# Parting the mixture's weights beside later attention heads, in a fixed place of each

## The chip, the cores and the metric

The kernel runs on one core of a Trainium2 chip. The metric is the device time of one execution in microseconds. Beside it stand profiles: one execution recorded by the hardware profiler, with the start and end of every instruction of each engine. PE is the matrix engine (PEld its weight loads), DVE the vector engine, ACT the scalar engine, POOL GpSimd, and SP the sync engine, which here only issues DMA transfers. Each engine takes its instructions from a queue of its own, in the order that the program gives it.

## The reference

The function is one transformer block with adaptive layer norm. `x` has 4 sequences of 512 tokens with 256 features.

```python
mod = (_silu(L0_c) @ L0_wmod).reshape(L0_c.shape[0], 6, 1, -1)
sa, ca, ga, sb, cb, gb = ...           # shifts, scales and gates of the two halves
h = _layernorm(x) * (1 + ca) + sa
x = x + ga * attention(h)              # 16 causal heads of 128, softmax in float32
h = _layernorm(x) * (1 + cb) + sb
x = x + gb * ffn(h)                    # 8 experts, top 2 by a router, and a shared one
```

The attention has 64 (sequence, head) pairs. The mixture of experts (`ffn`) takes `h` down to 128 features, sends every token through two of eight two-layer experts with hidden sizes of 128 to 512, adds a shared expert and a dense core, and goes back up to 256. All is float32.

## The kernel before, in words

**Float32 products in three passes.** A float32 operand is parted into a high part that the fast matmul format (`float32r`) holds and the rest: `hi = copy(a)`, `lo = a - hi`. A product is then three matmuls into one PSUM bank (`mm3`, lines 138 to 142: weights' rest, moving operand's rest, both high parts). Everything that meets a matmul this way is parted first: ACT copies, DVE or POOL subtracts (`rest`, line 148, so all subtractions carry that line and are told apart by their tiles).

**The attention loop** (lines 1028 to 1093) runs over the 64 pairs; index `n` is called a head here. Groups of four heads of one sequence follow each other: heads 0 to 3 are sequence 0, 4 to 7 sequence 1, and so on; heads 16 to 31 are the second group of weights. In head `n` the loop writes down

- the scores of the four token tiles (`weights`, lines 471 to 504). For each tile PE writes `ps` (lines 482 and 140 to 142), DVE masks it and finds the row's extreme (L488, which frees the PSUM bank; there are two of them), ACT takes the exponential (L498), DVE the reciprocal of the sum (L502), POOL multiplies by it (L503). The function hands out the instructions of each tile: `exp` is the exponential, `by_sum` the multiplication. Those of the fourth tile are the head's last.
- between the tiles, the projections `pq` and `pk` of the next head (`project`), then the values `pv` (`values`);
- the attention weights of this head transposed by DVE (L512, L518), four DMAs to DRAM (`moved`, L524) and one back (`aT`, L528);
- those of head `n - 2` parted (`parted`: ACT copies `aTh`, L535; POOL subtracts), those of head `n - 3` multiplied with the values (`pz`, then `zh` and `zl`), and those of head `n - 4` projected out (`po`).

**Weights of the attention** are loaded as they are needed (`load_unit`, lines 185 to 196): a DMA (L188) into a staging buffer, POOL copies (L194) and subtracts. The heads of sequence 3 load the query, key and value weights of the next group (heads 12 to 15, 28 to 31, 44 to 47); heads 16, 18, 32, 34, 48 and 50 load output weights.

**Weights of the mixture** are parted ahead, during the attention. There are 11 units of up to 128 x 512 (`TO_PART`: five "first", three "second", shared, core, down). `stage_wf` (lines 221 to 224) loads a unit by one to three DMAs (L182). `part_wf` (lines 226 to 237) parts it: an ACT copy into a second buffer (L234), a POOL subtraction in place (L148), and a DMA of each result to DRAM (L235, L237); a "second" unit is first also stored whole (L232), since the subtraction overwrites it. The parts are loaded back near the end of the attention. `PART_AT` says in which head a unit is parted; it is staged one head earlier.

**Buffers.** The staging tag "stage" has two buffers of 128 x 512 floats. `load_unit`'s block, a unit's block, and the unit's high part take them in turn, in the order in which the program writes them down. One comes free when its last reader is done: for a parted unit, when the DMA of the part has landed.

**What sets the order.** PE's queue follows the program's text. For the other engines a planner sorts the instructions at build time, by a simulated timeline: an instruction is put into its engine's queue where the simulation has the engine free and the operands ready, earlier text first. It can so stand well ahead of its place in the text. Two things hold it: data and buffers, and `tc.issue_after(i)`, under which every instruction written in the block is queued behind `i`, if it runs on `i`'s engine. Instructions of other engines in the block, DMAs of SP among them, are not held. At run time each queue is worked off in its order: an instruction that waits holds back what is queued behind it.

In the traced program L234 is the ACT copy of a unit; the first three run at 40 to 60 us, during heads 2 to 4, though the text has them at heads 7, 9 and 11.

Of the kernel before, what the change touches and what calls it, by code (L numbers as in the profile page):

```python
# [98 lines left out]


TO_PART = tuple(u for u, (_, in_parts) in UNITS.items() if in_parts)
PART_AT = (7, 9, 11, 20, 22, 24, 26, 36, 38, 40, 42)

LATE_UNITS = (
    ("first3", "wu", 0),
# [8 lines left out]
def adaln_attention_moe_kernel(  # L114
# [29 lines left out]
    def f32(a: bass.AP) -> bass.AP:  # L144
        return a.bitcast(F32)

    def rest(eng, lo, full, hi):
        return eng.tensor_tensor(lo, full, f32(hi), ALU.subtract)  # L148
# [30 lines left out]
    def load_runs(to: bass.AP, src: list):  # L179
        at = 0  # L180
        for a in src:
            nc.sync.dma_start(to[:, at : at + a.shape[-1]], a)  # L182
            at += a.shape[-1]

    def load_unit(src, nm: str, early: bool = False):

        st = work.tile([P, 512], F32, tag="stage", name=f"st_{nm}")
        nc.sync.dma_start(st, src)  # L188
        u = const.tile([P, 2, 512], F32R, tag="wu", name=nm, bufs=10)
        hi, lo = u[:, 0], u[:, 1]  # L190
        if early:
            nc.scalar.copy(hi, st)
        else:
            nc.gpsimd.tensor_scalar(hi, st, 1.0, 1.0, ALU.mult, ALU.mult)  # L194
        rest(nc.gpsimd, lo, st, hi)
        return hi, lo
# [19 lines left out]
    def wf_runs(u: str):  # L216
        return [wf[:, at * P : (at + n) * P] for at, n in runs(UNITS[u][0])]
# [3 lines left out]
    def stage_wf(u: str):  # L221
        n = len(UNITS[u][0]) * P
        staged[u] = work.tile([P, 512], F32, tag="stage", name=f"st_wf_{u}")[:, :n]
        load_runs(staged[u], wf_runs(u))

    def part_wf(u: str):

        n = len(UNITS[u][0]) * P
        st = staged[u]
        d = parts_d[u] = dram.tile([P, 3, n], F32, tag=f"wfp_{u}", name=f"wfp_{u}")  # L230
        if u.startswith("second"):
            nc.sync.dma_start(d[:, 2, :], st)  # L232
        hi = work.tile([P, 512], F32R, tag="stage", name=f"hi_wf_{u}")[:, :n]
        nc.scalar.copy(hi, st)  # L234
        nc.sync.dma_start(d[:, 0, :], f32(hi))  # L235
        rest(nc.gpsimd, st.bitcast(F32R), st, hi)
        nc.sync.dma_start(d[:, 1, :], st)  # L237
# [171 lines left out]
    def norm_batch(b: int, which: int):  # L409
        if which and b > 1:  # L410
            with tc.issue_after(recent["hidden"]):
                xns[b, which] = normed(b, which)
            return
        xns[b, which] = normed(b, which)
# [56 lines left out]
    def weights(b: int, h: int, q, k):  # L471


        e = work.tile([P, E_END], F32, tag="e", name=f"e_{b}_{h}")
        nm = small.tile([P, NT], F32, tag="nmax", name=f"nmax_{b}_{h}", bufs=4)
        tot = small.tile([P, NT], F32, tag="tot", name=f"tot_{b}_{h}", bufs=4)
        inv = small.tile([P, NT], F32, tag="inv", name=f"inv_{b}_{h}", bufs=4)
        for t in range(NT):
            n = (t + 1) * P
            ps = psum.tile([P, S], F32, tag="sc", name=f"ps_{b}_{h}_{t}")  # L480
            if t == 0:
                nc.tensor.matmul(ps[:, :n], lhsT=q[0], rhs=k[0], start=True, stop=True)  # L482
            else:
                at = ts(t - 1, P)
                mm3(ps[:, :n], (q[1][:, at], q[2][:, at]), (k[1][:, :n], k[2][:, :n]), True, True)
            et = e[:, E_AT[t] : E_AT[t] + n]

            least = nc.vector.tensor_tensor_reduce(  # L488
                out=et,
                in0=ps[:, :n],  # L490
                in1=maskf[:, S - n :],
                scale=-SCALE,
                scalar=BIG,
                op0=ALU.add,
                op1=ALU.min,
                accum_out=nm[:, t : t + 1],
            )
            exp = nc.scalar.activation(  # L498
                et, et, AF.Exp, bias=nm[:, t : t + 1], scale=-1.0, accum_out=tot[:, t : t + 1]
            )  # L500
            one = slice(t, t + 1)
            nc.vector.reciprocal(inv[:, one], tot[:, one])  # L502
            by_sum = nc.gpsimd.tensor_scalar(et, et, inv[:, one], 1.0, ALU.mult, ALU.mult)  # L503
            yield e, least.ins, exp.ins, by_sum.ins

    def turned(b: int, h: int, e):


        tb = work.tile([P, NB, X], F32, tag="T", name=f"T_{b}_{h}")
        blocks = e.rearrange("p (n i s) -> p n i s", i=NB, s=R)  # L510
        to = tb.rearrange("p i (n r) -> p n i r", r=R)
        nc.vector.transpose(to[:, 0], blocks[:, E_AT[0] // P])  # L512
        for c in range(NT):
            t = max(c, 1)
            n = NT - t
            first = PAIR_AT[c] + t - c
            at, step = E_AT[t] // P + c, E_STEP // P
            nc.vector.transpose(  # L518
                to[:, first : first + n], blocks[:, at : at + (n - 1) * step + 1 : step]
            )  # L520

        moved = dram.tile([NB, R, NB, X], F32, tag="moved", name=f"moved_{b}_{h}")
        for a in range(NB):
            nc.sync.dma_start(  # L524
                moved[:, :, a, :].rearrange("i s x -> s i x"), tb[a * R : (a + 1) * R]
            )
        aT = work.tile([P, NB, X], F32, tag="aT", name=f"aT_{b}_{h}", bufs=3)
        nc.sync.dma_start(aT, moved.rearrange("i s a x -> (i s) a x"))  # L528
        return aT
# [460 lines left out]
    def modulate(b: int, which: int):  # L990

        m = modulated(b, which)
        next(m)
        begun_norms.append(m)
# [33 lines left out]
    for n, (b, h) in enumerate(order):  # L1028
        scores = weights(b, h, q, k)
        nb, nh = order[n + 1] if n + 1 < N else (None, None)  # L1030
        next(scores)
        _, least, *_ = next(scores)

        if n < HG * (B - 1):
            if h == 0:
                with tc.issue_after(least):
                    norm_batch(b + 1, 0)
            if h == 2:
                modulate(b + 1, 0)
        if b == 0 and h < HG:  # L1040
            if h + 2 < HG:
                wqk_u[h + 2] = load_unit(wqk[h + 2], f"wqk{h + 2}")
            if h == 0:
                wv_u[1] = load_unit(wv[1], "wv1")
            if h in (1, 2):
                wo_u[h - 1] = load_unit(wo[h - 1], f"wo{h - 1}")
        for f, *args in later.pop(n, ()):
            f(*args)
        if n + 1 in PART_AT:
            stage_wf(TO_PART[PART_AT.index(n + 1)])  # L1050
        if n in PART_AT:
            part_wf(TO_PART[PART_AT.index(n)])
        if nb is not None:
            q = project(nb, nh, 0)
        next(scores)
        if nb is not None:
            k = project(nb, nh, 1)
        end_norm()
        e, _, exp, by_sum = next(scores)
        if len(waiting) > 1:  # L1060
            part_one(-2)
        if h % 2 == 0:
            values(b, h // 2, 1)
        elif nb is not None:
            values(nb, nh // 2, 0)
        else:
            last_exps["head"] = exp
            prepared[0] = before_chunks(0)
        if done:
            finish(n, *done.pop())  # L1070
        if len(waiting) == LAG:
            db, dh, aT = waiting.pop(0)
            done.append((db, dh, mixed(db, dh, aT)))
        with ExitStack() as after:
            if nb is None:
                after.enter_context(tc.issue_after(begun[0]))
            waiting.append((b, h, turned(b, h, e)))

        with tc.issue_after(by_sum):
            if b == B - 1 and h + HG < H:  # L1080
                wqk_u[h + HG] = load_unit(wqk[h + HG], f"wqk{h + HG}")
                if h % 2 == 0:
                    wv_u[(h + HG) // 2] = load_unit(wv[(h + HG) // 2], f"wv{(h + HG) // 2}")
            if b == 0 and h >= HG and h % 2 == 0:
                wo_u[h // 2] = load_unit(wo[h // 2], f"wo{h // 2}")
            if b == B - 1 and h + HG >= H:
                for u in (
                    ("down", "first0"),
                    ("whole", "second0"),
                    ("first1",),  # L1090
                    ("first2", "second1"),
                )[h + HG - H]:
                    load_wf(u)
# [6 lines left out]
    n = N  # L1100
# [97 lines left out]
```

## Time and profile before

| | |
|---|---|
| median of 3 runs | 817.98 us (817.22 to 819.26) |
| profiled execution | 815.89 us |
| its span, from the first to the last instruction | 814.1 us |
| mean granted clock of TensorE | 0.989 |
| busy: PE, DVE, ACT, POOL | 776.6, 596.6, 490.1, 520.6 us |
| a head with PE busy throughout (heads 24 to 34) | 9.19 us |
| DMA, hardware queue: share of the 16 engines' time, bytes moved | 52.4%, 123.21 MB |
| `moved` to landing, `aT` to landing (medians) | 2.8 and 4.0 us |

A profile's page gives the busy time of each engine, the waits between engines, and the chain of work that ended last. A table by stretches gives the same busy times for a part of the span, and a timeline the single instructions. In a line of waits, "A <- B: 8.8, 2, 4.5" says that A waited for B for 8.8 us in all, twice, 4.5 us at most. In a line of the timeline the first number is the start in us from the beginning of the span, the second the duration, and in brackets stands the engine's idle time before it and what ended it. Idle time of an engine that is not the bound costs nothing by itself.

The attention fills the first 628 us or so, the mixture of experts the rest.

### The profile page before, as it was taken

The numbers are of one execution on the slowest core, as the hardware profiler recorded it, in microseconds if no ns is written. First come the engines' busy times: TensorE is split into PE (matmuls) and PEld (weight loads), VectorE is DVE, ScalarE is ACT, GpSimd is POOL, SyncE is SP. The second block draws the span as 40 slices with busy tenths as digits, with TensorE's granted clock in tenths as the row PEclk, the third lists the DMA queues.
The fourth block names the chain that finished last, engine by engine and source line by source line (L and its number), as shares of the span: only waits on it lengthen the run. The fifth ranks groups of instructions, "written<-read, shape, count | busy, mean of one in ns | idle before, by whom it ended". The sixth has DMA issues, their size and how long they took to land.

```text
span 814.1 us, 14111 instructions
## 1 busy us (share of the span) xinstructions
PE 776.6 (95%) x4487; PEld 671.2 (82%) x4487; DVE 596.6 (73%) x1734; ACT 490.1 (60%) x1184; POOL 520.6 (64%) x523
## 2 busy tenths in 40 slices
PE   6898999999999999999999999999998998989997
PEld 5677898999978999998899999999887766767775
DVE  5976888777657777766777677778898587795555
ACT  3575667666656765665666666666656334656663
POOL 4665566896756688675656886656556245565675
PEclk9999999999999999999999999999999899999999
DMA  7376454665775456657555675644576333322221
GB/s 234 102 254 190 130 156 132 183 184 155 219 229 158 135 171 186 179 159 209 160 145 159 174 194 146 186 132 140 153 195 206 105 123 85 101 57 74 57 82 61
DMA packets 73218, 124.12 MB, mean 152 GB/s; under 512 B 8996, under 2 KB 51252, under 8 KB 73144
## 3 DMA queue, kind: packets, MB, share of 16 engines
q1 hardware_dynamic: 73112, 123.21, 52.4%
q8 instruction: 36, 0.59, 0.3%
q14 instruction: 38, 0.31, 0.1%
q0 software_dynamic: 32, 0.02, 0.0%
HBM read 73.05 MB, written 50.14 MB: 151 GB/s over the span
## 4 chain that ended last, share of the span: by engine, by line
PE 72%; DVE 10%; DMA 7%; POOL 4%; ACT 2%; issue 2%; SPq 2%; DVEq 0%; ACTq 0%; POOLq 0%
PE acc L835 4%; PE ps L140 3%; PE pz L140 3%; PE pz L141 3%; PE pz L142 3%; PE ps L141 3%; PE ps L142 3%; PE po L140 3%; PE po L141 3%; PE po L142 3%; PE pk L141 3%; PE pk L140 3%; PE pk L142 3%; PE pv L140 3%; PE pv L142 3%; PE pv L141 3%
## 5 line engine op out<-in xcount | busy, mean ns | idle before, releaser
L148 POOL TENSOR_TENSOR aT<-aT,aTh 128x1152 fp32r<-128x1152 f32 x64 | 172.0, 2687 | 109.0 <-ACT aTh L535 105.9
L503 POOL TENSOR_SCALAR e<-e,inv 128x128 f32<-128x128 f32 (+3 forms) x256 | 135.1, 542 | 68.7 <-DVE inv L502 66.2
L498 ACT ACTIVATE e<-e,nmax 128x128 f32<-128x128 f32 (+3 forms) x256 | 143.3, 561 | 49.7 <-DVE nmax L488 48.9
L535 ACT CAST aTh<-aT 128x1152 fp32r<-128x1152 f32 x64 | 74.0, 1157 | 122.8 <-DMA aT<-moved 61.9
L488 DVE CUSTOM_DVE_ANT_0 e<-ps,mask 128x128 f32<-128x128 f32 (+3 forms) x256 | 120.3, 478 | 28.6 <-PE ps L482 17.8
L518 DVE STREAM_TRANSPOSE T<-e 128x384 f32<-128x384 f32 (+2 forms) x256 | 100.5, 445 | 10.2 <-POOL e L503 10.1
L140 PE MATMUL ps<-kh,ql 128*128 128x256 f32 (+2 forms) x192 | 71.6, 373 | 12.4 <-DVE nmax L488 12.4
L148 DVE TENSOR_TENSOR zl<-pz,zh 128x512 fp32r<-128x512 f32 x64 | 43.9, 687 | 48.9 <-ACT zh L553 48.2
L140 PE MATMUL po<-wo,zl 128*128 128x256 f32 x256 | 73.1, 286 | 1.0 <-DVE zl L148 1.0
L140 PE MATMUL pv<-wv,hTl 128*128 128x256 f32 x256 | 72.0, 281 | 0.5 <-DVE hTl L148 0.5
L141 PE MATMUL po<-wo,zh 128*128 128x256 f32 x256 | 72.1, 282 | 0.0
L142 PE MATMUL po<-wo,zh 128*128 128x256 f32 x256 | 72.0, 281 | 0.0
L141 PE MATMUL pv<-wv,hTh 128*128 128x256 f32 x256 | 71.5, 279 | 0.0
L142 PE MATMUL pv<-wv,hTh 128*128 128x256 f32 x256 | 71.5, 279 | 0.0
L502 DVE RECIPROCAL inv<-tot 128x1 f32<-128x1 f32 x256 | 40.2, 158 | 40.8 <-ACT e L498 33.6
L863 POOL TENSOR_TENSOR oacc<-oacc,part 128x512 f32<-128x512 f32 x28 | 40.9, 1461 | 43.4 <-DVE part L859 36.5
L141 PE MATMUL ps<-kl,qh 128*128 128x256 f32 (+2 forms) x192 | 65.4, 340 | 0.3 <-DVE kl L148 0.3
L140 PE MATMUL pz<-aTh,vl 128*128 128x512 f32 (+2 forms) x192 | 65.0, 339 | 0.0
L141 PE MATMUL pz<-aT,vh 128*128 128x512 f32 (+2 forms) x192 | 64.9, 338 | 0.0
L142 PE MATMUL ps<-kh,qh 128*128 128x256 f32 (+2 forms) x192 | 64.9, 338 | 0.0
L142 PE MATMUL pz<-aTh,vh 128*128 128x512 f32 (+2 forms) x192 | 64.9, 338 | 0.0
L140 PEld LDWEIGHTS ps<-kh,ql 128*128 128x128 f32 x192 | 36.5, 190 | 22.3 <-DVE nmax L488 15.3
(216 smaller groups left out, 2332.1 us busy)
## 6 DMA issues: line engine op xcount, KB each, us to landing
moved<-T SPq DMA_DIRECT2D x256, 160.0 KB, 2.8
aT<-moved SPq DMA_DIRECT2D x64, 640.0 KB, 4.0
spread<-gates_e SPq DMA_DIRECT2D x32, 256.0 KB, 3.3
st_wqk<-in_wqk SPq DMA_DIRECT2D x16, 256.0 KB, 3.7
wf_first<-wfp_first SPq DMA_DIRECT2D x5, 512.0 KB, 4.7
st_wv<-in_wv SPq DMA_DIRECT2D x8, 256.0 KB, 3.3
st_wo<-in_wo SPq DMA_DIRECT2D x8, 256.0 KB, 3.4
wmod<-in_wmod SPq DMA_DIRECT2D x6, 256.0 KB, 5.6
```

What stands on the lines that cost most here:

```text
L140: nc.tensor.matmul(o, lhsT=wl, rhs=mh, start=start, stop=False)
L141: nc.tensor.matmul(o, lhsT=wh, rhs=ml, start=False, stop=False)
L142: nc.tensor.matmul(o, lhsT=wh, rhs=mh, start=False, stop=stop)
L148: return eng.tensor_tensor(lo, full, f32(hi), ALU.subtract)
L488: least = nc.vector.tensor_tensor_reduce(out=et, in0=ps[:, :n], in1=maskf[:, S - n :], scale=-SCALE, scalar=BIG, op0=ALU.add, op1=ALU.min, ...
L498: exp = nc.scalar.activation(et, et, AF.Exp, bias=nm[:, t : t + 1], scale=-1.0, accum_out=tot[:, t : t + 1])
L502: nc.vector.reciprocal(inv[:, one], tot[:, one])
L503: by_sum = nc.gpsimd.tensor_scalar(et, et, inv[:, one], 1.0, ALU.mult, ALU.mult)
L518: nc.vector.transpose(to[:, first : first + n], blocks[:, at : at + (n - 1) * step + 1 : step])
L535: nc.scalar.copy(hi, full)
L835: nc.tensor.matmul(acc, lhsT=w2(k, b), rhs=act[:, s], start=c == 0, stop=c == n - 1)
L863: recent["added"] = nc.gpsimd.tensor_tensor(oacc, oacc, to, ALU.add).ins
```

## The change

The list of heads in which units are parted changes from 7, 9, 11, 20, 22, 24, 26, 36, 38, 40, 42 to 18, 20, 22, 24, 26, 28, 34, 36, 38, 40, 42. The first three partings leave the first twelve heads; two come to heads 18 and 28 and one to head 34, and the units move along in their order.

The two calls move within the head's text, from ahead of the next head's query projection to behind the DVE transposes of the head's own weights. They stand under two `issue_after`: the ACT copy is queued behind the head's last exponential, the POOL subtraction behind the head's last normalisation. The DMAs of staging and storing are held by neither, since they run on SP.

```diff
-PART_AT = (7, 9, 11, 20, 22, 24, 26, 36, 38, 40, 42)
+PART_AT = (18, 20, 22, 24, 26, 28, 34, 36, 38, 40, 42)
...
         for f, *args in later.pop(n, ()):
             f(*args)
-        if n + 1 in PART_AT:
-            stage_wf(TO_PART[PART_AT.index(n + 1)])
-        if n in PART_AT:
-            part_wf(TO_PART[PART_AT.index(n)])
         if nb is not None:
             q = project(nb, nh, 0)
...
             waiting.append((b, h, turned(b, h, e)))
+
+        with tc.issue_after(by_sum), tc.issue_after(exp):
+            if n + 1 in PART_AT:
+                stage_wf(TO_PART[PART_AT.index(n + 1)])
+            if n in PART_AT:
+                part_wf(TO_PART[PART_AT.index(n)])
 
         with tc.issue_after(by_sum):
             if b == B - 1 and h + HG < H:
```

## The prediction

> **What bounds the kernel now.** I read the page first, for the busiest engine; then a table by stretches, for where that engine stands idle; then the waits and the chain inside the bad stretches, and the timeline of a good one. Part 1 of the page:
>
> ```profile
> PE 776.6 (95%) x4487; PEld 671.2 (82%) x4487; DVE 596.6 (73%) x1734; ACT 490.1 (60%) x1184; POOL 520.6 (64%) x523
> ```
>
> PE is the bound, so only its idle time can be won: 814.1 - 776.6 = 37.5 us. The stretches are cut at the first score matmul (L482) of a head: heads 4 to 5, 19 to 23, 24 to 34, 35 to 40.
>
> ```profile
> 54.80:78.50 23.70, 18.82 (x118) 16.56 (x117) 16.27 (x56) 14.10 (x36) 14.03 (x13) 1.00 0.69 204
> 202.40:252.30 49.90, 47.15 (x292) 42.02 (x292) 32.21 (x105) 30.73 (x81) 32.14 (x33) 1.00 0.70 211
> 252.30:353.40 101.10, 101.10 (x640) 92.24 (x639) 75.20 (x240) 64.48 (x171) 73.55 (x77) 1.00 0.58 165
> 353.40:411.80 58.40, 56.24 (x350) 50.22 (x350) 40.20 (x130) 36.11 (x97) 37.62 (x39) 1.00 0.63 180
> ```
>
> The columns are length, then busy time of PE, PEld, DVE, ACT, POOL. Heads 24 to 34 leave PE no gap: 101.1 / 11 = 9.19 us a head. Against it heads 19 to 23 are 49.9 - 5 x 9.19 = 3.95 too long, heads 35 to 40 58.4 - 6 x 9.19 = 3.26, and in heads 4 to 5 PE stands 23.70 - 18.82 = 4.88. Sum 12.1 us. These are the stretches of the partings: the eleven L234 copies run at 40.5, 50.5, 59.7 (heads 2 to 4), 204.5, 212.3, 221.6, 233.6 (19 to 22), 355.0, 364.3, 369.5 and 378.3 us (35 to 37), earlier than the heads they are written beside, since only data and buffers hold them. Waits in 202 to 252 us (total, times, longest):
>
> ```profile
> POOL st_wf_second L148 <- DMA wfp_second<-st_wf_second: 8.8, 2, 4.5
> DVE zl L148 <- ACT zh L553: 8.3, 5, 3.1
> ...
> ACT hi_wf_second L234 <- DMA st_wf_second<-in_wf: 5.5, 2, 3.0
> ...
> PE ps L140 <- DVE nmax L488: 2.6, 3, 1.2
> ```
>
> The copy stands in ACT's queue before its block has landed. The whole softmax queues behind it: ACT, then DVE's reduction L488, whose score bank PE needs. The chain in order of time goes through the parting itself:
>
> ```profile
> 218.65 2.76 DMA st_wf_second<-in_wf
> 221.64 0.62 ACT hi_wf_second L234
> ...
> 228.96 4.58 DMA st_wf_second<-in_wf
> 233.61 2.33 DMA wfp_second<-st_wf_second
> 236.11 1.29 POOL st_wf_second L148
> 237.40 2.66 POOL aT L148
> ```
>
> Now a clean head without parting (26), ACT and POOL around its last exponential and last normalisation:
>
> ```profile
> 276.25 0.72 ACT L498 ACTIVATE e<-e,nmax 128x512 f32<-128x512 f32 x1 [0.61 <-DVE nmax L488]
> ...
> 280.06 1.16 ACT L535 CAST aTh<-aT 128x1152 fp32r<-128x1152 f32 x1 [1.88 <-DMA aT<-moved]
> ...
> 277.35 0.69 POOL L503 TENSOR_SCALAR e<-e,inv 128x512 f32<-128x512 f32 x1 [1.29 <-DVE inv L502]
> 281.30 2.69 POOL L148 TENSOR_TENSOR aT<-aT,aTh 128x1152 fp32r<-128x1152 f32 x1 [3.25 <-ACT aTh L535]
> ```
>
> Behind them ACT idles 1.88 us and POOL 3.25 us, both for the attention weights' round trip through DRAM.
>
> **What the Trainium skill says.** "TensorE: Matmul & The Clock Gate", the table at its head: the queues of ScalarE, VectorE and GpSimdE are strict FIFOs. The trace agrees: nothing of ACT runs in the 2.97 us before 221.64. "DMA: Bandwidth & Descriptors", Rules for kernel authors: issue a DMA early, wait for it late. The trace shows both ways: copies at 204.5 and 355.0, whose blocks had landed 14 to 15 us before, waited 0.0; the ones at 212.3 and 221.6, each issued within 0.3 us of its landing, stood 3.06 and 2.97. The same page, "Issuing engines are not separate DMA queues": all transfers share the same 16 engines. Agreed: `aT` takes 4.0 us in the median, 5.17 beside a parting's traffic (58.0 us).
>
> **The change part by part.** No instruction is added or removed: still 11 copies (0.62 us, two of 0.41), 11 subtractions (1.30, two of 0.74), the same loads and stores (256 KB in some 3 us).
>
> 1. *Partings leave heads 2 to 4.* Waits of 1.74, 1.50 and 1.85 us before the copies go, and three subtractions of 1.3 us on POOL. The PE gaps of 1.47 (58.4 us) and 3.41 (71.2 us) follow them; the second comes through `aTh` (63.22) to POOL's `rstd`, DVE's `xn`, L488. Heads 8 and 9 hold the same layer norm of another sequence, no parting, and no gap. I take off 4.9, and leave 0.7, a fifth of 3.41, for the layer norm itself; bounds 0 and 3.4.
>
> 2. *Copies behind the head's last exponential, subtractions behind its last normalisation.* The block, staged by a DMA that is not tied to either, can land well before. So the ACT waits (3.06, 2.97, 2.57, 4.03, 1.84) and POOL waits (4.25, 4.53) go. 0.62 fits into ACT's 1.88 and 1.30 into POOL's 3.25. Queued behind the copy are `vh`, `aTh`, `zh` and the next head's exponentials; behind the subtraction `aT`'s, needed a head later. Without this cover each would move the next head's L488. That one has room: in head 27 DVE idles 0.71 us before it and it ends at 280.64, while PE wants its bank at 281.89: 1.25 + 0.71 = 1.96 us, more than either. Two precedents without a wait, at 204.5 and 355.0, are followed by heads of 9.19. I take off 3.95 + 3.26 and put back 0.1 for each of 11 partings, 1.1; bounds 0 and 1.5 each.
>
> 3. *The stores and loads on SP.* Each parting issues two stores (three for a "second" unit) in SP's queue, shared with `moved` and `aT`. A load whose buffer still waits for such a store stops those behind it: SP stood 3.2 us at L188 for `wfp_down` before 385.5, and heads 38 and 40 lost 0.91 and 0.82. The last parting moves to 42 and the next loads, `wqk` and `wv` of heads 12 on, still follow it. I leave half of 1.73, 0.9; bounds 0 and 1.7.
>
> 4. *Two "stage" buffers.* In heads 18, 28 and 34 a head's weights now follow a parting. At 28 `wqk` and `wv` were loaded at 238 us, 58 us ahead of their POOL work (296.4); now they wait until both stores land, some 6 us after the exponential, then 3.5 us for their own. POOL may stop for a landing: 3.5 - 1.96 = 1.5 us a place at worst, zero if it is busy meanwhile. I take 1.0 for the three places; bounds 0 and 4.5. Their use is two heads (18 us) later.
>
> Sum: -12.1 + 0.7 + 1.1 + 0.9 + 1.0 = -8.4. The profiled execution took 815.89 (span 814.1 and 1.8 around it): 807.5, a span of 805.7. The three runs have a median of 817.98, 2.1 above it: 809.6.
>
> **Rivals.** *Only the early heads gain* (0.15): a parting in every second head keeps SP and DMA late there, and the 7.2 us of heads 19 to 40 come back at 18 to 43. What is left is 4.9 - 0.7 = 4.2: 813.8. For it, DMA is at 0.70 and 0.63 in the parted stretches against 0.58; against it, the two precedents.
>
> *Nothing moves* (0.10): head 5's 3.41 is the layer norm's own and the waits reappear on SP: 1.5 of gain from 58.4, about 1 lost: 817.5. For it, the last links before that gap are `rstd` and `xn`; against it, heads 8 and 9.
>
> *Slower* (0.15), one mechanism: POOL's 1.3 us plus 0.6 of DMA crowding delay `aT`, the next normalisations and the transposes by 1.9 us, just the room of 1.96, so a little more lateness stops PE in every parted head. At 1.5 us each (heads 22 and 23 lost 1.6 and 2.3) 11 x 1.5 = 16.5 against 11.4 saved: 823.1. It decides from 11.4 / 11 = 1.04 us a parting. Against it stands POOL's 64% load.
>
> **How the numbers follow.** My forecast has 0.60; alone it spans 806 (all 12.1 won) to 813. The range 805 to 819 leaves out most of the slower case and a little below. A measurement of this kernel tells some 0.3%, 2.5 us. Faster: 0.58 + 0.12 = 0.70; same: 0.02 + 0.03 + 0.08 = 0.13; slower: 0.17 (that rival and the tail of the others).
>
> **What would show it.** Right: no L234 copy before 190 us; none with a DMA wait of over 0.5 us; each within 2 us behind its head's last exponential; heads 4, 5, 22, 23 and 37 near 9.2 to 9.4; PE idle near 29 us. Wrong: new PE waits for L488 in heads 18 to 30 or 34 to 43; longer SP waits at L188 or L182; POOL stopping at L194 for `st_wqk`, `st_wv` or `st_wo`; `aT` landing over 5 us after issue. The forecast fails if the fixed place makes ACT or POOL wait for something else.

## The result, and the profile after

The kernel after takes 810.73 us (median of 5 executions, 809.29 to 813.81) against 817.98 (817.22 to 819.26): a ratio of 0.9927, 95% interval 0.9906 to 0.9947. The profiled execution took 809.29 us with a span of 807.5, 6.6 us shorter than before. 809.6 us was forecast, and a span of 805.7.

Part 1 of the page of the kernel after, the busy time of the engines:

```profile
PE 775.5 (96%) x4487; PEld 671.9 (83%) x4487; DVE 594.7 (74%) x1734; ACT 490.9 (61%) x1184; POOL 521.7 (65%) x523
```

PE's work is the same; its idle time fell from 37.5 to 807.5 - 775.5 = 32.0 us. The table by stretches of the kernel after, cut at the same heads as in the prediction (4 to 5, 19 to 23, 24 to 34, 35 to 40); the columns are length, then busy time of PE, PEld, DVE, ACT and POOL, then TensorE's granted clock, the DMA share and GB/s:

```profile
55.60:78.20 22.60, 20.55 (x119) 18.03 (x119) 18.59 (x61) 12.86 (x34) 13.49 (x15) 0.92 0.51 145
201.70:247.60 45.90, 45.90 (x292) 41.91 (x291) 33.28 (x107) 30.14 (x79) 31.96 (x32) 1.00 0.65 198
247.60:349.10 101.50, 101.42 (x640) 92.08 (x639) 71.36 (x236) 65.76 (x175) 76.34 (x78) 1.00 0.65 192
349.10:404.20 55.10, 55.10 (x350) 50.32 (x349) 40.55 (x133) 36.12 (x96) 39.08 (x40) 1.00 0.63 189
```

Heads 19 to 23 went from 49.9 to 45.9 us and heads 35 to 40 from 58.4 to 55.1: 9.18 us a head, PE without a gap. Heads 24 to 34, which now hold four partings (24, 26, 28, 34), grew by 0.4 only. Where the span's 6.6 us come from, by the first score matmul of each head:

| | before | after | difference |
|---|---|---|---|
| start to head 0 | 20.2 | 19.5 | -0.7 |
| heads 0 to 10 | 108.7 | 108.7 | 0.0 |
| heads 11 to 18 | 73.5 | 73.5 | 0.0 |
| heads 19 to 23 | 49.9 | 45.9 | -4.0 |
| heads 24 to 34 | 101.1 | 101.5 | +0.4 |
| heads 35 to 40 | 58.4 | 55.1 | -3.3 |
| head 41 to the end | 402.3 | 403.3 | +1.0 |

So all of the gain is in heads 19 to 40, and the early heads, from which the forecast took half of its gain, gave nothing.

The waits of the kernel after in heads 19 to 23, the longest three (total, times, longest):

```profile
POOL aT L148 <- ACT aTh L535: 9.9, 5, 4.3
ACT aTh L535 <- DMA aT<-moved: 5.6, 3, 3.5
DVE zl L148 <- ACT zh L553: 5.1, 5, 1.7
```

The waits of ACT for `st_wf_second`, of POOL for `wfp_second` and of PE for L488 are gone. What is left is the attention weights' own round trip. The timeline of the kernel after around the parting of head 22 (ACT, then POOL):

```profile
235.67 0.73 ACT L498 ACTIVATE e<-e,nmax 128x512 f32<-128x512 f32 x1 [0.69 <-DVE nmax L488]
...
236.40 0.61 ACT L234 CAST hi_wf_first<-st_wf_first 128x512 fp32r<-128x512 f32 x1
...
238.46 1.16 ACT L535 CAST aTh<-aT 128x1152 fp32r<-128x1152 f32 x1 [0.32 <-PE pz L142]
...
236.78 0.69 POOL L503 TENSOR_SCALAR e<-e,inv 128x512 f32<-128x512 f32 x1 [1.05 <-DVE inv L502]
237.44 1.30 POOL L148 TENSOR_TENSOR st_wf_first<-st_wf_first,hi_wf_first 128x512 fp32r<-128x512 f32 x1
239.69 2.70 POOL L148 TENSOR_TENSOR aT<-aT,aTh 128x1152 fp32r<-128x1152 f32 x1 [0.96 <-ACT aTh L535]
```

The copy stands right behind the exponential with no idle time before it, and so do all eleven, at 198.7, 217.9, 236.4, 253.9, 274.3, 292.3, 347.1, 365.6, 384.7, 401.6 and 420.7 us. The copy and the subtraction lie in time in which ACT and POOL waited for `aT` and `aTh` before (1.88 and 3.25 us in head 26 of the kernel before); ACT's wait before `aTh` is 0.32 us here and POOL's before `aT` 0.96, and PE stops nowhere in this head.

### The profile page after: what moved, and what is told of

Read it like the earlier page. It is cut to its first block, busy times and chain, and to the rows that moved or that the text cites. A ratio compares the mean times of both kernels' runs of the same rounds, so it can differ in the third digit from the quotient of the medians.

```text
span 807.5 us, 14122 instructions
## 1 busy us (share of the span) xinstructions
PE 775.5 (96%) x4487; PEld 671.9 (83%) x4487; DVE 594.7 (74%) x1734; ACT 490.9 (61%) x1184; POOL 521.7 (65%) x523
## 5 line engine op out<-in xcount | busy, mean ns | idle before, releaser
L488 DVE CUSTOM_DVE_ANT_0 e<-ps,mask 128x128 f32<-128x128 f32 (+3 forms) x256 | 120.1, 478 | 23.8 <-PE ps L482 14.6
L140 PE MATMUL po<-wo,zl 128*128 128x256 f32 x256 | 73.1, 285 | 0.6 <-DVE zl L148 0.6
L863 POOL TENSOR_TENSOR oacc<-oacc,part 128x512 f32<-128x512 f32 x28 | 40.9, 1462 | 43.5 <-DVE part L859 36.8
L592 POOL TENSOR_TENSOR x<-x,tmp 128x512 f32<-128x512 f32 x32 | 41.4, 1298 | 19.7 <-DVE tmp L590 19.5
```

The costliest lines, as they stand in the source:

```text
L140: nc.tensor.matmul(o, lhsT=wl, rhs=mh, start=start, stop=False)
L488: least = nc.vector.tensor_tensor_reduce(out=et, in0=ps[:, :n], in1=maskf[:, S - n :], scale=-SCALE, scalar=BIG, op0=ALU.add, op1=ALU.min, ...
L592: nc.gpsimd.tensor_tensor(xu, xu, tmp, ALU.add)
L863: recent["added"] = nc.gpsimd.tensor_tensor(oacc, oacc, to, ALU.add).ins
```

## The experiments

The kernel before had a median of 816.89 us beside the first four, 817.17 beside the next four and 816.67 beside the last three. "Heads 0 to 10" is from the first score matmul to that of head 11; "heads 18 to 43" has 26 x 9.19 = 238.9 us of work. Both are of one profiled execution each. Up to the start of head 11, six of the kernels (after, list_only, no_pin, rest_pin, copy_pin, mid_pin) ran the same instructions in the same order on every engine. Their 107.3 to 111.6 us in heads 0 to 10 show by how much single profiles of one program differ there; the largest belongs to the slowest of no_pin's 17 executions.

| kernel | median us | ratio to before, 95% interval | heads 0 to 10 | heads 18 to 43 |
|---|---|---|---|---|
| before | 817.98 | | 108.7 | 246.1 |
| after | 810.73 | 0.9927 [0.9906, 0.9947] | 108.7 | 239.3 |
| list_only | 818.58 | 1.0028 [1.0015, 1.0041] | 107.5 | 249.0 |
| no_pin | 820.04 | 1.0038 [1.0024, 1.0052] | 111.6 | 250.2 |
| pin_only | 809.50 | 0.9907 [0.9887, 0.9927] | 108.5 | 239.3 |
| rest_pin | 809.64 | 0.9908 [0.9893, 0.9923] | 107.3 | 240.7 |
| copy_pin | 810.94 | 0.9933 [0.9915, 0.9952] | 109.6 | 239.1 |
| mid_pin | 815.53 | 0.9985 [0.9970, 1.0000] | 109.0 | 244.1 |
| kh_first | 808.45 | 0.9902 [0.9885, 0.9919] | 107.5 | 240.7 |
| gates_later | 808.22 | 0.9901 [0.9883, 0.9920] | 107.9 | 240.6 |
| late_loads | 809.98 | 0.9913 [0.9889, 0.9937] | 109.7 | 241.7 |
| early_both | 807.57 | 0.9885 [0.9863, 0.9906] | 105.8 | 239.9 |
| all_early | 806.18 | 0.9869 [0.9846, 0.9891] | 105.6 | 241.7 |

### The list of heads, and the fixed place, each alone

**list_only** is the kernel before with the new list `PART_AT` and nothing else; **pin_only** is the kernel after with the old list.

> The kernel before with the new list of heads alone: same place in the text, nothing held. Theory (the gain is the fixed place of the copies behind the last exponential): the copies still run ahead of their heads, ACT waits for blocks in flight, PE loses some 5 to 8 us in heads 17 to 43; 815 to 819 us. Rival (the gain is the list: one parting in every second head, none in the first twelve): 809 to 812 us. Early heads: as in the changed kernel, no parting before head 14.

> The changed kernel with the old list of heads: partings at 7, 9, 11, 20 and so on, each behind its head's last exponential and normalisation. Theory: heads 19 to 23 and 35 to 40 cost 9.19 us each, no copy waits for its block by more than 0.5 us; 809 to 813 us. Rival (the list): 815 to 819 us. For the early heads: if the partings of heads 2 to 4 cost 4 us of their own, this kernel, which has them at heads 7 to 11, shows heads 2 to 5 without the gaps; if those gaps belong to the start of the pipeline, 4 to 6 us of PE idle stay there.

The list alone makes the kernel slightly slower. Its copies, written in heads 18 to 42, run ahead again: 185.1, 203.6, 211.1, 219.9, 226.6, 235.1 us and, later, 339.4 to 379.5 us. Waits of list_only from 190 to 425 us, the two that matter:

```profile
PE ps L140 <- DVE nmax L488: 7.0, 8, 1.9
...
ACT hi_wf_first L234 <- DMA st_wf_first<-in_wf: 5.5, 2, 2.7
```

Heads 21 to 24 take 10.51, 9.75, 11.43 and 11.33 us there. The fixed place alone, with the old list, gives all of the gain: heads 18 to 43 are as clean as in the kernel after. With the first partings held to heads 7, 9 and 11, heads 0 to 10 take the same 108.5 us in all, but not in the same places. PE's idle time in heads 2 to 5 falls to 3.24 us (6.75 in the kernel before, 5.01 in the kernel after), between the two outcomes that were expected, and heads 6 to 10 take 52.4 us instead of 50.0.

### No fixed place, or only one of its two ties

**no_pin** is the kernel after without either `issue_after`; **copy_pin** ties the ACT copy alone, **rest_pin** the POOL subtraction alone.

```diff
-        with tc.issue_after(by_sum), tc.issue_after(exp):
+        if True:                          # no_pin
+        with tc.issue_after(exp):         # copy_pin
+        with tc.issue_after(by_sum):      # rest_pin
```

> The changed kernel without both issue_after: new list, new place in the text, nothing held. Theory: the copies move ahead again and wait for their blocks; 814 to 819 us. Rival (the later place in the text is enough, since earlier text goes first): 809 to 812 us.

> The changed kernel with only the copy held, behind the last exponential, and POOL's subtraction free. The planner makes the same queues of it on every engine as with both, so it must take the changed kernel's time, 809 to 812 us, and shows by how much two measurements of one program differ; if it differs by more than 2 us from 810.7, smaller differences in this study say nothing.

> The changed kernel with POOL's subtraction held behind the last normalisation but ACT's copy free. Theory (the copy at the head of ACT's queue is what costs): several copies wait 1 to 4 us for their block again, 812 to 818 us. Rival (POOL's wait for the store and the subtraction in its queue is what costs): 809 to 812 us.

no_pin is again slower than before, 1.0 us above what the theory allowed. Its trace has the same instructions in the same order on every engine as that of list_only: without a tie, the planner makes the same queues from either place in the text, so the new place by itself does nothing. As repetitions of one program the two medians, 818.58 and 820.04 us, lie 1.5 us apart. copy_pin has the same queue on every engine as the kernel after, so it is a repetition of that one: 810.94 us.

rest_pin missed the theory and took the time of its rival. Its copies are free to run ahead, and seven of the eleven wait, two of them marked as for their block (1.32 and 3.70 us), but the median is that of the kernel after. The timeline of ACT in rest_pin, around its longest such wait:

```profile
354.81 0.19 ACT L498 ACTIVATION_READ_ACCUMULATOR e<-e,nmax 128x1 f32 x1
...
359.17 0.62 ACT L234 CAST hi_wf_second<-st_wf_second 128x512 fp32r<-128x512 f32 x1 [3.70 <-DMA st_wf_second<-in_wf]
359.69 1.15 ACT L535 CAST aTh<-aT 128x1152 fp32r<-128x1152 f32 x1
...
361.23 0.40 ACT L498 ACTIVATE e<-e,nmax 128x128 f32<-128x128 f32 x1
```

A wait of 3.70 us cost its head 9.77 - 9.19 = 0.58 us. The prediction's own figures come near it: the wait and the copy are 3.70 + 0.62 = 4.32 us, ACT's usual idle time there is 1.88 and the next L488 has room of 1.96; 4.32 - 3.84 = 0.48 is left (an estimate). The sum isn't exact: for a wait of 1.32 us at 281.0 it gives nothing, and head 28 took 9.89 us, 0.70 more than a clean one. Both are small. In rest_pin the copies run at least 15 us apart. In list_only and no_pin they crowd, 5 to 9 us apart: five fall into heads 19 to 22 and four into heads 35 to 37, and list_only's heads from 21 to 24 and from 36 to 40 lose up to 2.2 us each. So a single wait in a queue hardly costs, and the crowding of the partings is the likeliest cause of the loss; either tie ends it. It was not tried by itself: rest_pin fixes the subtraction's place too, so POOL's queue, the rival, stays possible. A part of that rival can be left out. The subtractions' waits for stores, 8.8 us in the kernel before, are all but absent from list_only and no_pin (one, of 0.55 us or less in each), and both lose more than the kernel before.

### Another fixed place

**mid_pin** ties both behind the second tile's exponential and normalisation instead of the fourth's.

```diff
-        _, least, *_ = next(scores)
+        _, least, exp_2, sum_2 = next(scores)
...
-        with tc.issue_after(by_sum), tc.issue_after(exp):
+        with tc.issue_after(sum_2), tc.issue_after(exp_2):
```

> The changed kernel with copy and subtraction held behind the second tile's exponential and normalisation, so in the middle of the head, with the block long landed. Theory A (what costs is a copy that waits for its block): no ACT wait, 809 to 812 us. Theory B (what costs is the place: 0.62 us of ACT ahead of the third and fourth exponential and 1.30 us of POOL ahead of their normalisations): up to 11 x 0.6 = 6.6 us more, 814 to 818 us.

It keeps about a fifth of the gain. The time falls into the range of theory B, but not by its mechanism: no copy waits for its block, and eight of the eleven heads with a parting take 9.19 us. The excess is in heads 30 (10.81), 32 (10.73) and 37 (10.15). The chain that ended last in mid_pin at head 30, in order of time (start, length, what):

```profile
299.24 0.62 POOL wqk L194
299.85 2.65 POOL aT L148
302.51 1.25 POOL wqk L148
303.75 0.59 POOL wv L194
304.34 1.38 POOL e L503 x3
305.72 1.26 POOL wv L148
306.98 0.68 POOL e L503
307.66 0.02 issue
307.68 1.56 DVE T L518 x4
309.24 0.31 DVE e L488
```

POOL works without a break from 299.24 to 307.66 us: the parting of two units of the attention's own weights stands between and ahead of the normalisations `e`. These come late, then DVE's transposes, then L488, and PE stands 1.36 us before 309.62. In the waits from 190 to 425 us, POOL's stops at L194 for a weight load add up to 6.6 + 5.9 us in mid_pin:

```profile
POOL wo L194 <- DMA st_wo<-in_wo: 6.6, 2, 4.0
POOL wqk L194 <- DMA st_wqk<-in_wqk: 5.9, 2, 5.0
```

In the kernel after it is one line of 1.6 us. The place of the parting also sets when the shared staging buffers come free, and with them where the attention's weights land. That the buffers are what differs at head 30 was only read off these lines; it was not tried by itself.

### The early heads

The window table of the kernel before for heads 0 to 3 and 6 to 10, and then that of the kernel after for heads 0 to 10, 0 to 3 and 4 (same columns as above):

```profile
20.20:54.80 34.60, 31.48 (x170) 25.94 (x169) 29.31 (x95) 22.15 (x60) 23.00 (x29) 0.95 0.53 162
78.50:128.90 50.40, 50.15 (x324) 45.23 (x323) 41.91 (x132) 32.44 (x84) 29.14 (x32) 1.00 0.51 144
```

```profile
19.50:128.20 108.70, 101.90 (x608) 89.51 (x607) 88.29 (x282) 67.88 (x178) 63.00 (x70) 0.97 0.51 141
19.50:55.60 36.10, 31.64 (x169) 26.13 (x168) 28.78 (x95) 22.41 (x60) 21.72 (x27) 0.95 0.55 150
55.60:69.00 13.40, 11.35 (x61) 9.63 (x61) 10.75 (x37) 6.88 (x19) 8.74 (x10) 0.87 0.51 148
```

PE's idle time in heads 0 to 3 grew from 34.60 - 31.48 = 3.12 to 36.10 - 31.64 = 4.46 us; in heads 4 and 5 it fell from 4.88 to 22.60 - 20.55 = 2.05. Over heads 0 to 10 it fell from 3.12 + 4.88 + 0.25 = 8.25 to 6.80, but PE's busy time rose by the same 1.45. Two things took the place of what was removed.

*New waits.* The timeline of the kernel after in heads 2 and 3 (SP's issues, ACT, DVE, PE):

```profile
36.76 0.65 SPq L188 DMA_DIRECT2D st_wqk<-in_wqk  x1
37.51 0.61 SPq L188 DMA_DIRECT2D st_wv<-in_wv  x1
39.26 0.33 SPq L528 DMA_DIRECT2D aT<-moved  x1
...
44.66 1.16 ACT L535 CAST aTh<-aT 128x1152 fp32r<-128x1152 f32 x1 [2.02 <-DMA aT<-moved]
...
45.88 0.59 ACT L467 CAST kh<-pk 128x512 fp32r<-128x512 f32 x1
...
46.50 0.69 DVE L148 TENSOR_TENSOR kl<-pk,kh 128x512 fp32r<-128x512 f32 x1 [2.84 <-ACT kh L467]
...
47.19 0.67 DVE L488 CUSTOM_DVE_ANT_0 e<-ps,mask 128x512 f32<-128x512 f32 x1
...
48.01 0.36 PE L140 MATMUL ps<-kh,ql 128*128 128x256 f32 x1 [1.49 <-DVE nmax L488]
```

With the mixture's units gone the staging buffers are free, and the weights of heads 12 on, loaded at 63.9 and 66.9 us before, are loaded at 36.8 and 37.5. The first `aT` behind them takes 39.26 to 44.64, 5.4 us. Its copy `aTh` stands in ACT's queue ahead of the keys' copy `kh`; DVE's `kl` waits 2.84 us for that, and L488 behind it makes PE wait. In all six kernels with these queues the first `aT` takes 5.0 to 5.4 us; in before, pin_only and late_loads, where the loads come later, it takes 3.9 to 4.0.

The next gap of PE, 1.91 us before 60.11, comes from the second `aTh` by a longer way (ACT, POOL, POOL, DVE, DVE):

```profile
53.11 1.16 ACT L535 CAST aTh<-aT 128x1152 fp32r<-128x1152 f32 x1 [1.72 <-DMA aT<-moved]
54.35 2.68 POOL L148 TENSOR_TENSOR aT<-aT,aTh 128x1152 fp32r<-128x1152 f32 x1 [1.98 <-ACT aTh L535]
57.00 1.27 POOL L503 TENSOR_SCALAR e<-e,inv 128x384 f32<-128x384 f32 x2
58.30 1.56 DVE L518 STREAM_TRANSPOSE T<-e 128x384 f32<-128x384 f32 x4 [0.87 <-POOL e L503]
59.78 0.26 DVE L488 CUSTOM_DVE_ANT_0 e<-ps,mask 128x128 f32<-128x128 f32 x1
```

`aTh` waits 1.72 us for its transfer and POOL's subtraction waits for `aTh`. Two normalisations stand in POOL's queue behind that subtraction, DVE's transposes wait for them, and L488 stands behind the transposes.

The kernel before has the same link in its own gaps. For the one of 1.47 us (ACT, DVE, PE):

```profile
55.05 1.16 ACT L535 CAST aTh<-aT 128x1152 fp32r<-128x1152 f32 x1 [1.85 <-DMA aT<-moved]
56.95 0.16 DVE L502 RECIPROCAL inv<-tot 128x1 f32<-128x1 f32 x1 [3.14 <-ACT e L498]
58.37 0.45 PE L140 MATMUL ps<-kh,ql 128*128 128x384 f32 x1 [1.47 <-DVE nmax L488]
```

ACT's last exponential of the head stood behind the `aTh` of 55.05, which waited for its transfer and not for a parting. The gap of 3.41 us goes through the `aTh` of 63.22, which waited 1.46 us for its own. Whether partings made those transfers late earlier on is not shown.

*A slower clock.* The timeline of PE in the kernel after behind that second gap:

```profile
60.11 0.45 PE L140 MATMUL ps<-kh,ql 128*128 128x384 f32 x1 [1.91 <-DVE nmax L488]
...
61.20 0.57 PE L142 MATMUL pk<-hTh,wqk 128*128 128x512 f32 x1
61.57 0.63 PE L140 MATMUL pk<-hTh,wqk 128*128 128x512 f32 x1
62.00 0.63 PE L141 MATMUL pk<-hTl,wqk 128*128 128x512 f32 x1
```

The matmuls of 512 columns start 0.43 us apart instead of 0.23 until 64 us. The granted clock of 60 to 65 us is 0.66, a loss of 5 x 0.34 = 1.7 us. The kernel before has one such spell in these heads (39 to 43 us), the kernel after two (37 to 41 and 61 to 65), and so has its repetition copy_pin.

Five kernels, each with one or more edits to the kernel after, were made to tell which operand is the late one. **kh_first** queues `aTh` behind `kh` in heads 0 to 7:

```diff
-            part_one(-2)
+            with ExitStack() as after:
+                if n < 8:
+                    after.enter_context(tc.issue_after(recent["k"]))   # the last kh
+                part_one(-2)
```

**gates_later** writes the gates' products of the layer norm two heads later:

```diff
-    later[1] = [(make_gates,)]
+    later[3] = [(make_gates,)]
...
-        later[2 + b] = [(gate_attention, b)]
-    later[2 + B] = [(modulation, 1)]
+        later[4 + b] = [(gate_attention, b)]
+    later[4 + B] = [(modulation, 1)]
```

**late_loads** ties the loads of the next group's weights behind an earlier `aT` (`backs` holds the `aT` transfers, L528, in order):

```diff
-        with tc.issue_after(by_sum):
+        with tc.issue_after(by_sum), tc.issue_after(backs[n - 4] if B * HG > n >= 4 else by_sum):
             if b == B - 1 and h + HG < H:
```

**early_both** has the first two, **all_early** all three.

> The changed kernel, and in heads 0 to 7 the ACT copy of the attention weights (aTh) is queued behind the copies of the next head's keys (kh). In heads 2 to 4 of the changed kernel aTh stands ahead of kh and waits 1.7 to 3.0 us for the transfer aT, and PE stops behind it. Theory (that order in ACT's queue is what takes the place of the partings' waits): the gap of 1.49 us at 48 us and a part of those in head 4 go, 2 to 5 us less than the changed kernel, 805 to 809 us. Rival (the first heads wait for the transfer itself, in whatever order): same time, 809 to 812 us.

> The changed kernel with the gates computed two heads later (at head 3 instead of 1; their loads and the second modulation follow). Their DVE work, 1.5 us and more, stands beside the PE gap of 1.22 us at 37 us that every kernel of this study has. Theory (that work is the gap's cause): the gap goes, about 1 us less, 808 to 811 us, or it moves to head 4. Rival (the gap is the start of the pipeline): it stays.

> The kernel after, with one tie more: in heads 12 to 15 the loads of the next group's weights stand on SP behind the aT transfer of four heads before. In the kernel after, the first of them ran at 36.8 and 37.5 us, just ahead of the aT of 39.26 that took 5.38 us and stood behind the PE gaps at 48.0 (1.49 us). Theory, the transfers that moved into the place of the mixture's units are what took the early gain: no load of st_wqk or st_wv before 80 us, the first aT lands in about 4 us, the gap at 48 us falls to under 0.5 and the one at 60 us to under 1; first score matmul to the start of head 11 goes from 108.7 to about 106 us, the median to 808. Rival, the order on ACT alone makes the gaps: 108.2 to 109.2 us and 810 to 811.5 us, with the waits for aT as long as in the kernel after.

> The kernel after, with both edits of the heads before head 8: the copy of the attention weights (aTh) behind the copy of the next head's keys (kh) in heads 0 to 7, and the gates computed two heads later. Each alone moved a gap instead of removing it (medians of 808.45 and 808.22 us against 810.73). If their gains add, the first score matmul to the start of head 11 takes about 105 us and the median is 806 us. If each gap only moves on to the next late operand, 107 to 108.7 us and 808 to 810 us.

> All three early edits together: aTh behind kh, gates two heads later, loads of the next group's weights behind an earlier aT. Heads 0 to 10 at 9.19 us each would take 101.1 us, against 108.7 in the kernel after. If the early gaps are late operands that these three put right, about 103.5 us and a median of 805 us; if PE there always finds another operand late, over 106.5 us and 808 us or more.

kh_first cuts the gap at 48 us from 1.49 to 0.62, and PE then stands 2.86 us before 59.60. gates_later removes the gap of 1.22 us at 37, as its theory had it, and PE then stands elsewhere, 1.78 us before 34.2 and 2.25 before 80.4. Both medians are some 2.4 us below that of the kernel after, measured beside other runs of the kernel before, with overlapping intervals.

late_loads was right on the place and wrong on the sum. SP and ACT in late_loads:

```profile
39.55 0.34 SPq L528 DMA_DIRECT2D aT<-moved  x1
...
43.56 1.16 ACT L535 CAST aTh<-aT 128x1152 fp32r<-128x1152 f32 x1 [0.24 <-DMA aT<-moved]
...
54.84 1.15 ACT L535 CAST aTh<-aT 128x1152 fp32r<-128x1152 f32 x1 [4.56 <-DMA aT<-moved]
```

With the loads moved to 116 us the first `aT` takes 4.0 us instead of 5.4 and the gap at 48 us is gone. This agrees with what the Trainium skill says in "DMA: Bandwidth & Descriptors", "Issuing engines are not separate DMA queues": transfers run on the same engines and interleave. Its other half, that the issuing engine doesn't matter, no run here shows, since all of these transfers come from SP. But the next `aT` is waited for 4.56 us and PE stands 1.50 us before 56.2, head 4 takes 12.32 us with a spell of slow clock from 59 to 62, head 6 loses 1.3 us to a late modulation, and heads 0 to 10 take 109.7. So the displaced loads made one gap, and removing it left the total within the scatter of the six. They are not the only thing that can delay the first `aT`: in all_early it takes 5.1 us without them, beside the `moved` transfers of the next head.

The two order edits together bring heads 0 to 10 to 105.8 us, all three to 105.6: below all six profiles of the unedited queues, and 3 us less than the kernel after, two thirds of what the forecast took off. all_early still has a gap of 3.25 us at 47.6 and one of 1.76 at 34.3. It beats both kernels: 806.18 us, 0.9869 of before, its interval below that of the kernel after. What the third edit adds to early_both (807.57) is within the intervals. Its heads 18 to 43 took 2.4 us more than those of the kernel after; this was not followed up.

## Why the prediction was right, and where it was wrong

The time came out 1.1 us above the forecast. That it came so near is partly luck: part 1 took off 4.2 us that did not come, and the other three parts gained 2.7 us more than they were given.

**Part 1, the early heads: predicted -4.2, measured 0.0. This step failed.** It took PE's 4.88 us of idle time in heads 4 and 5 as caused by the partings and removable with them, because the gaps follow the partings' waits in time. What links them to PE in the trace, as the prediction notes for the second, is `aTh`, which waits for the attention weights' own transfer: 1.85 and 1.46 us in the kernel before, and still 2.02, 1.72 and 2.95 for the first three of the kernel after, without any parting. In heads 4 and 5 the idle time did fall, by 2.8. But the step looked at these two heads alone, not at heads 0 to 3, where idle time rose by 1.3, and put the removal of the staging at nothing: loads moved into the freed buffers, and the first `aT` behind them was late. The 1.45 us of idle time that was saved in all went into a second spell of slow clock, which no term of the sum had. The six profiles of these queues show 107.3 us at the least, where the forecast asks for 104.5. That heads 8 and 9 hold the same layer norm without a gap showed that it makes none by itself in a full stretch, not that heads 4 and 5 have none without partings. The prediction named a landing of `aT` over 5 us as a sign against it; that sign came, at 39.26, in the heads where it was not looked for.

**Part 2, the fixed place: predicted -7.21 and +1.1 back; measured -4.0 and -3.3, and 0.0 back.** The waits in heads 19 to 23 and 35 to 40 were all removable, and 0.62 us on ACT and 1.30 on POOL do fit into the idle time before `aTh` and `aT`. The 0.1 a parting was caution without a mechanism. Of the room of 1.96 us that was read from head 27, rest_pin says both: 3.70 us of waiting cost 0.58, which fits it, and 1.32 us cost 0.70, which doesn't.

**Part 3, stores and loads on SP: predicted +0.9, measured +0.3.** Heads 38 and 40 take 9.19 us with a parting's stores beside them, so stores alone do not make their 0.91 and 0.82 of before. The mechanism shows once, behind the parting of head 24: SP stood 2.24 us at L182, before 258.88, until a store of `wfp_first` had landed. `moved` stood behind it, `aT` was issued at 264.32, and `aTh` ran at 268.36 after a wait of 4.74. The lateness reached PE at 277.38, where it waited some 0.3 us for L488; that is the 9.52 us of head 27. This chain was read from the trace, not tried.

**Part 4, the two buffers: predicted +1.0, measured +0.1.** The heads behind 18, 28 and 34 show no gap. POOL stopped for loads of `wqk` for 1.6 us in all, in heads 29 and 30; head 30 takes 9.29. In mid_pin such stops add up to 12.5 us; in the kernel after the term was small.

The sum by terms: predicted -8.4, measured 0.0 - 7.3 + 0.3 + 0.1 = -6.9, and +0.3 outside the heads named (-0.7 ahead of head 0, +1.0 behind head 40): -6.6. The median then lay 1.4 us above the profiled execution, where 2.1 was assumed.

**The rivals.** *Only the early heads gain* is the reverse of what happened: only the later heads gained. *Nothing moves* was right for the early heads, though not by its reason (head 5 takes 9.19 us now and the layer norm is not the gap), and wrong for heads 19 to 40. *Slower*, with a cost of over 1.04 us for each of 11 partings, had one small sign: the 0.3 us of head 27, behind the parting of head 26. No other head from 18 to 43 loses more than 0.1 us.

What stays open is which operand bounds heads 2 to 6 in the end. Each edit alone moved PE's idle time to other places, two together won 3 us, and the slow spells come and go with them. The layer norm's share was not taken apart.

## What to carry to other kernels

When work is moved out of a stretch with several late operands, list what is queued behind it on each engine, DMA queues too, and ask which of them is the next late one; only if none is within the gain may it be counted. A stretch in which PE already ran without a gap beside the same work is a much better precedent than a gap that merely follows the work. And a planner that lets side work run ahead can do harm, here most likely by crowding it: holding it to the end of each head, by a tie on either of its engines, was worth 7 us, and in the middle of the head 1.6, while the choice of the heads was worth nothing.

## What was not expected of the hardware

The clock's slow spells in the middle of a busy kernel. In heads 0 to 10 one lasts 3.41 us at half speed (61 to 65 us in the kernel after: 0.63, 0.50, 0.50, 0.66 a microsecond) and costs 1.7 us. The Trainium skill, "TensorE: Matmul & The Clock Gate", Part 1, has the half rate and the window of about 3.4 us, and puts the drop after an idle window of that length. Length and rate agree. The cause is wider here: PE needn't be idle for a whole window.

The traces show more than that. In each of the 13, every stretch of full or half clock except the one that the end cuts off lasts a whole number of times 3.41 us. So a trace can be laid out in windows of that length, and each window's busy share of PE set beside the clock of the window that follows:

| kernel | window (us) | PE busy | clock in the next window |
|---|---|---|---|
| after | 34.0 to 37.4 | 0.20 | half |
| after | 57.8 to 61.3 | 0.44 | half |
| before | 35.6 to 39.0 | 0.55 | half |
| before | 66.3 to 69.7 | 0.44 | full |
| before | 69.7 to 73.1 | 0.56 | full |

In all 13 traces, from the first full clock at 17 to 19 us on, 47 windows at full clock have a busy share under 0.43, and half clock follows each of them. Of 32 windows from 0.44 to 0.58 it follows 12, and of 2852 windows above that none. So the limit lies near half, and a gap counts by how much of one window it takes. The gap of 1.91 us in the kernel after lies in one window; the gap of 3.41 us in the kernel before is divided between two, and brought no spell. This was read from the traces, not tried by an edit.

Heads 0 to 10 hold no spell in rest_pin; one each in before, list_only, pin_only, gates_later and all_early; two each in after, copy_pin, kh_first, late_loads and early_both; one of double length in mid_pin, and one single and one double in no_pin. Six of these ran the same queues, and the windows lie differently against the kernel in each execution. So in a stretch with gaps of 1 to 3 us, 1.7 us more or less hang on where the gaps fall in the windows, which no sum of waits contains.
